# Four of 22 tile lists moved from layer 0 into layer 1's loop, with small steps given to ScalarE and GpSimd

## The chip, the cores and the metric

One core of a Trainium2 chip runs the whole program. The time is that of the device in microseconds, the median of several runs. Engines are named as the profile does: PE is TensorE's matmul and PEld its weight load, DVE is VectorE, ACT ScalarE, POOL GpSimd, SP SyncE, which here only issues transfers.

## The reference, cut to what matters

Four graph layers run one after the other on N = 2708 nodes with D = 128 features and one adjacency matrix `adj` of 2708 x 2708, of which under 1% is not zero. Each layer normalises x, takes the ReLU, and adds its result to x.

```python
# layer 0
msg = jnp.matmul(H.T, X); msg * inv_deg[:, None]
# layer 1
messages = gelu(s[:, None, :] + d[None, :, :] + msg_b)
aggregated = jnp.einsum('ijd,ij->id', messages, adj)
new_feats = concatenate([node_feats, aggregated]) @ upd_w.T + upd_b
# layer 2: adj @ states, then a GRU cell
# layer 3: two heads of attention, masked by adj > 0
```

Layer 1 needs one Gelu for each pair (i, j) and feature, but only where adj[i, j] is not zero.

## The kernel before, in words

The rows are 22 tiles of 128 (the last has 20), in groups of four (`GROUPS`). For layer 1 the columns are cut into 22 blocks of JB = 124. In each block the kernel keeps up to S = 8 entries of each row: `val` (their values) and `col` (their column numbers), made by `max` and `max_index` on VectorE. These are the lists. The diagonal is kept apart: `own` has its values, and `near` is a copy of the two or three blocks around the diagonal with the diagonal set to zero.

**Layer 0** (lines 173 to 234) reads adj tile by tile into `a4`, which holds four tiles and exists twice. For each tile PE adds to the six accumulators `accs`; GpSimd makes `near` and `dg` (the diagonal); VectorE sums `dg` to `own` (L211) and makes the 22 blocks of the list (L216, L217); ScalarE counts the entries by `Sign` (L219). For each group PE transposes 22 x 4 squares (L225), ScalarE evacuates them to `aT` and sums them into `sums` (L229), and SP stores them in `adjT` (L232) for layer 2. Loads and stores stand in one queue, SP's. The order of the instructions in this part is made by the framework's own scheduler. After it VectorE makes `deg` from `sums` (L239 to L243), which `enter` needs.

**Layer 1** is written out by hand under `manual_schedule`: each engine's queue has the order of the program text. First the steps `enter`, `rows_and_turn`, `turn_rows` and `destinations` bring in the six groups, with the periods -3, -2, -1 between them; then `period(t)` runs for t = 0 to 22, and the rest of `updates`. A period works on several tiles at once, in six steps k = 0 to 5:

- `combine(t, k)`: PE adds source and destination parts of four blocks in a bank `p_m` (two banks); `activate(t, k)`: ScalarE's Gelu (L511); `gather(t, k)`: PE multiplies by `put` and adds to `agg`.
- `put_values(t + 1)`, at the start: GpSimd makes the first HP = 8 blocks of `put` from `mine` and `value` (L423). `put_more(t + 1, k)`: ScalarE makes the other 14 (L431).
- `pass_on(t + 1)` and `columns(t + 1)`: the column numbers go through DRAM and come back spread over the partitions.
- `rank(t + 3)` and `describe(t + 3)`, at k = 1: PE counts (`p_r`), VectorE copies the counts to `ends` and `ends4`; then `split` cuts `val` in three bf16 parts: ScalarE casts (L324), VectorE subtracts (L325, `v_r`), ScalarE casts (L326), GpSimd subtracts (L327).
- `select_rows(t + 3)` at k = 2 compares for `sel` and shifts it by one partition through SP to `later`; `finish_rows(t + 3)` at k = 4 subtracts (L370).
- `fetch(t + 2)` at k = 1 and 2: PE fetches the entries by `sel`; `place(t + 2)` at k = 3: VectorE makes `slot`, `hot`, `picked`, `where`, `value` and `mine`.
- `count_rows(t + 4)` at k = 2 reads the list of tile t + 4: the list has to be there by then.
- `sources` every second period and `updates` in steps over eight periods.

**Layers 2 and 3** follow, with `layer3_weights` making `w_x` and `src_w`. A dense version of all layers stands behind a test and isn't run here.

Of the kernel before, what the change touches and what calls it, by code (L numbers as in the profile page):

```python
# [20 lines left out]
F32 = mybir.dt.float32  # L21
BF16 = mybir.dt.bfloat16
AF = mybir.ActivationFunctionType
ALU = mybir.AluOpType
# [6 lines left out]
P = 128  # L31
# [20 lines left out]
def size(t):  # L52
    return min(P, N - t * P)


def width(b):
    return min(JB, N - b * JB)
# [3 lines left out]
def listed_layers(ctx: ExitStack, tc: tile.TileContext, x, adj, w, out, flag):  # L61
# [8 lines left out]
    def bank(name):  # L70
        return ps.tile([P, CH], F32, tag="ps", name=name)
# [98 lines left out]

    sumT = keep.tile([D, N], F32, name="hT1")
    hT = sumT
    with tc.tile_pool(name="l0c", bufs=1) as fix:
        offdiag = fix.tile([P, P], F32, name="offdiag")
        nc.vector.tensor_scalar(offdiag, ident, -1.0, 1.0, ALU.mult, ALU.add)
        sums = fix.tile([P, NT, len(GROUPS)], F32, name="sums")
        nc.gpsimd.memset(sums, 1.0)
        with (
            tc.tile_pool(name="l0", bufs=2) as rows,
            tc.tile_pool(name="l0k", bufs=2) as pool,  # L180
            tc.tile_pool(name="l0t", bufs=4) as turned,
            tc.tile_pool(name="l0p", bufs=1, space=PSUM) as acc,
        ):
            accs = [acc.tile([P, CH], F32, name=f"acc{c}") for c in range(len(CHUNKS))]
            for gi, (g0, gk) in enumerate(GROUPS):
                i0, iw = span(g0, gk)
                a4 = rows.tile([P, 4, N], F32, name="a")
                if gk < 4:
                    nc.gpsimd.memset(a4[:, gk - 1, :], 0.0)
                for q in range(gk):  # L190
                    n = g0 + q
                    m = size(n)
                    a = a4[:, q, :]
                    nc.sync.dma_start(a[0:m, :], adj[n * P : n * P + m, :])
# [5 lines left out]
                    d0 = n * P  # L200
                    b0 = d0 // JB
                    b1 = (d0 + m - 1) // JB
                    c0, c1 = b0 * JB, min((b1 + 1) * JB, N)
                    near = pool.tile([P, 3 * JB], F32, name="near")
                    nc.gpsimd.tensor_copy(near[:, 0 : c1 - c0], a[:, c0:c1])
                    dg = pool.tile([P, P], F32, name="dg")
                    nc.gpsimd.tensor_tensor(dg[:, 0:m], a[:, d0 : d0 + m], ident[:, 0:m], ALU.mult)
                    nc.gpsimd.tensor_tensor(
                        near[:, d0 - c0 : d0 - c0 + m], a[:, d0 : d0 + m], offdiag[:, 0:m], ALU.mult
                    )  # L210
                    nc.vector.reduce_sum(own[:, n : n + 1], dg[:, 0:m], AX.X)  # L211
                    for b in range(NB):
                        ab = a[:, b * JB : b * JB + width(b)]
                        if b0 <= b <= b1:
                            ab = near[:, b * JB - c0 : b * JB - c0 + width(b)]
                        nc.vector.max(val[:, n, b, :], ab)  # L216
                        nc.vector.max_index(col[:, n, b, :], val[:, n, b, :], ab)  # L217
                    sign = pool.tile([P, N], BF16, name="sign")
                    nc.scalar.activation(sign, a, AF.Sign, accum_out=total[:, n : n + 1])  # L219
                for j in range(NT):  # L220
                    k = size(j)
                    p = bank("p_T")
                    for q in range(gk):
                        m = size(g0 + q)
                        nc.tensor.transpose(  # L225
                            p[0:k, q * P : q * P + m], a4[0:m, q, j * P : j * P + k], ident[0:m, 0:m]
                        )
                    aT = turned.tile([P, CH], F32, name="aT")
                    nc.scalar.activation(  # L229
                        aT[0:k, 0:iw], p[0:k, 0:iw], AF.Copy, accum_out=sums[0:k, j, gi : gi + 1]  # L230
                    )
                    nc.sync.dma_start(adjT[0:k, j, i0 : i0 + iw], aT[0:k, 0:iw])  # L232
# [6 lines left out]
        nc.vector.reduce_sum(dsum, sums, AX.X)  # L239
# [15 lines left out]
    nc.vector.tensor_scalar(half_b, b_hh[:, 2:3], 0.5, None, ALU.mult)  # L255


    NX = 2 * D + 4
    w_x = late.tile([P, NX], F32, name="w_x")
    src_w = late.tile([P, 2, P], F32, name="src_w")  # L260

    def layer3_weights():
        nc.vector.tensor_copy(w_x[:, 0 : 2 * D], ff0T)
        for k in range(2):
            p = bank("p_w")[:, 0:2]
            nc.tensor.matmul(p, ff0[:, k, :], attn[:, 2 * k : 2 * k + 2], start=True, stop=True)
            nc.vector.tensor_copy(w_x[:, 2 * D + k : 2 * D + k + 1], p[:, 1:2])
            nc.vector.tensor_copy(w_x[:, 2 * D + 2 + k : 2 * D + 3 + k], p[:, 0:1])
        for k in range(2):
            nc.vector.tensor_copy(src_w[:, k, :], w_x[:, 2 * D + 2 + k : 2 * D + 3 + k].to_broadcast([P, P]))  # L270

    HB = NB // 2
    HP = 8
    R = 4
    C = 4 * S + R + 1  # L280
    with (
# [2 lines left out]
        tc.tile_pool(name="l1w", bufs=1) as once,  # L284
        tc.tile_pool(name="l1s", bufs=4) as selpool,
        tc.tile_pool(name="l1b", bufs=3) as three,
        tc.tile_pool(name="l1q", bufs=2) as putpool,
        tc.tile_pool(name="l1y", bufs=2, space=PSUM) as ypool,
        tc.tile_pool(name="l1m", bufs=2, space=PSUM) as mpool,
# [29 lines left out]
        for q in range(2):  # L319
            nc.vector.tensor_copy(xb[q][:, :, 4 * S : 4 * S + R], part.unsqueeze(1).to_broadcast([P, NB, R]))  # L320

        def split(dst, src, rest):

            nc.scalar.copy(dst[0], src)  # L324
            nc.vector.tensor_tensor(rest, src, dst[0], ALU.subtract)  # L325
            nc.scalar.copy(dst[1], rest)  # L326
            nc.gpsimd.tensor_tensor(dst[2], rest, dst[1], ALU.subtract)  # L327

# [8 lines left out]
        def compare(dst, numbers, op):  # L337
# [5 lines left out]
                op,  # L343
            )

        def rank(t):
            p = rpool.tile([P, CH], F32, tag="r", name="p_r")
            nc.tensor.matmul(p[:, 0:NB], before, rows_n[:, t, :], start=True, stop=True)
            nc.vector.tensor_copy(ends[:, t, :], p[:, 0:NB])
            nc.vector.tensor_copy(ends4, p[:, 0:NB].unsqueeze(2).to_broadcast([P, NB, R]))  # L350

        def describe(t):
            x = xb[t % 2]
            rest = once.tile([P, NB, S], F32, name="v_r")
            split([x[:, :, q * S : (q + 1) * S] for q in range(3)], val[:, t, :, :], rest)
# [30 lines left out]
        def place(t):  # L386
# [70 lines left out]
        def sources(k):  # L457
# [24 lines left out]
            gs = three.tile([P, 2, D], F32, name="gs")  # L482
# [113 lines left out]
        def period(t):  # L596
# [5 lines left out]
            for k in range(GB):  # L602
# [131 lines left out]
    row = l3.tile([P, 2, N], F32, name="row")  # L734
    score = l3.tile([P, NT, 4], F32, name="score")
    nc.gpsimd.memset(score[:, NT - 1, :], 0.0)
    ident_8 = l3.tile([P, P], U8, name="ident_8")
    nc.vector.tensor_copy(ident_8, ident)
    PIECE = 5
    RUNS = ((0, 3), (3, 8), (11, 8), (19, 3))  # L740
    MOST = 8
# [781 lines left out]
```

## Time and profile before

| | us |
|---|---|
| median of 3 runs | 1118.6 (1118.3 to 1119.38) |
| profiled execution | 1119.5 |
| its span, first to last instruction | 1117.6 |
| PE, PEld busy | 966.6, 763.3 |
| DVE, ACT, POOL busy | 840.2, 504.0, 393.4 |
| layer 0, first load to `deg` | 0.7 to 242.0 |
| entry of layer 1, to PE's first combine | 242.0 to 313.7 |
| loop of layer 1 | 313.7 to 652 |
| layers 2 and 3 | 652 to 1117.6 |

Busy times are sums over the span and overlap between engines. A group's row gives the line, the engine, the operation, the tiles written and read, the number of instructions, the busy time and the mean of one. In a timeline the columns are the start in us, the length, the engine and line; a bracket has the idle time ahead of the instruction and what ended it. In a list of waits they are the total in us, the number and the longest.

### The profile page before, as it was taken

The numbers are of one execution on the slowest core, as the hardware profiler recorded it, in microseconds if no ns is written. First come the engines' busy times: TensorE is split into PE (matmuls) and PEld (weight loads), VectorE is DVE, ScalarE is ACT, GpSimd is POOL, SyncE is SP. The second block draws the span as 40 slices with busy tenths as digits, with TensorE's granted clock in tenths as the row PEclk, the third lists the DMA queues.
The fourth block names the chain that finished last, engine by engine and source line by source line (L and its number), as shares of the span: only waits on it lengthen the run. The fifth ranks groups of instructions, "written<-read, shape, count | busy, mean of one in ns | idle before, by whom it ended". The sixth has DMA issues, their size and how long they took to land. (4 is left out here: it accounts for less than half of the span.)

```text
span 1117.6 us, 21914 instructions
## 1 busy us (share of the span) xinstructions
PE 966.6 (86%) x7968; PEld 763.3 (68%) x7968; DVE 840.2 (75%) x2948; ACT 504.0 (45%) x1319; POOL 393.4 (35%) x466
## 2 busy tenths in 40 slices
PE   3988887932489999999999988999979999999993
PEld 1554444512379999989898953444468899999772
DVE  5999999997647667687777364656668987997673
ACT  3966656622556666666665631433322200230143
POOL 3111112102546656666665343354301200250132
PEclk9999898755589999999999988999989999999996
DMA  9497886521113332232332046555300000000000
GB/s 357 187 312 261 309 294 241 186 61 51 53 56 102 106 105 102 82 106 79 105 105 79 28 144 211 186 198 199 99 18 1 1 9 1 1 20 1 2 15 14
DMA packets 55298, 125.39 MB, mean 112 GB/s; under 512 B 7414, under 2 KB 19782, under 8 KB 52472
## 3 DMA queue, kind: packets, MB, share of 16 engines
q1 hardware_dynamic: 48590, 121.12, 31.2%
q10 hardware_dynamic: 6590, 2.77, 1.0%
q8 instruction: 64, 1.05, 0.4%
q14 instruction: 54, 0.44, 0.1%
HBM read 77.30 MB, written 30.84 MB: 97 GB/s over the span
## 5 line engine op out<-in xcount | busy, mean ns | idle before, releaser
L804 PE MATMUL att<-hv,wt 128*128 128x129 f32 (+2 forms) x1936 | 240.7, 281 | 9.2 <-DVE wt L772 9.2
L804 PEld LDWEIGHTS att<-hv,wt 128*128 128x128 f32 (+2 forms) x1936 | 221.8, 190 | 26.3 <-DVE wt L772 8.7
L772 DVE SCALAR_TENSOR_TENSOR wt<-row,lift,mask 128x1024 f32<-128x1024 f32 (+5 forms) x176 | 160.0, 939 | 34.2 <-PE att L804 34.1
L423 POOL TENSOR_SCALAR put<-mine,value 128x128 f32<-128x128 bf16 x176 | 144.8, 839 | 74.2 <-DVE mine L339 71.8
L499 PE MATMUL p_m<-s,sel 128*128 128x128 bf16 x1452 | 161.9, 220 | 7.7 <-ACT g L511 4.7
L503 PE MATMUL p_m<-d,cols 124*128 124x128 bf16 (+1 forms) x1452 | 161.7, 219 | 1.4 <-DVE cols L453 1.3
L119 POOL TENSOR_TENSOR n_r<-n_r,minus_half 128x4 f32<-128x4 f32 (+1 forms) x36 | 48.3, 1343 | 298.5 <-DVE n_r L118 289.6
L196 PE MATMUL acc<-a,hs 128*128 128x512 f32 (+2 forms) x264 | 122.3, 599 | 24.7 <-DMA a<-in_adj 17.9
L524 PE MATMUL agg<-put,g 128*128 128x128 f32 (+1 forms) x968 | 135.9, 281 | 0.0
L925 PE MATMUL p_agg<-a,hs 128*128 128x512 f32 (+2 forms) x264 | 111.1, 562 | 8.2 <-DVE u L572 4.1
L524 PEld LDWEIGHTS agg<-put,g 128*128 128x128 f32 x968 | 118.2, 192 | 0.0
L217 DVE FIND_INDEX8 col<-val,a 128x8 uint16<-128x124 f32 (+1 forms) x441 | 117.9, 278 | 0.0
L499 PEld LDWEIGHTS <-sel 128*128 128x128 bf16 x1452 | 104.1, 98 | 13.3 <-issue 9.5
L503 PEld LDWEIGHTS <-cols 124*128 124x128 bf16 (+1 forms) x1452 | 102.3, 98 | 2.5 <-DVE cols L453 1.9
L511 ACT ACTIVATE g<-p_m 128x512 f32<-128x512 f32 x132 | 73.0, 553 | 65.6 <-PE p_m L503 64.5
L216 DVE MAX8 val<-a 128x8 f32<-128x124 f32 (+1 forms) x441 | 101.8, 269 | 0.0
L431 ACT ACTIVATE put<-mine,value 128x128 f32<-128x128 bf16 x308 | 100.5, 390 | 0.0
L225 PEld LDWEIGHTS p_T<-ident,a 128*128 128x128 f32 x484 | 59.6, 147 | 56.3 <-ACT aT L229 27.0
L196 PEld LDWEIGHTS acc<-a,hs 128*128 128x128 f32 (+1 forms) x264 | 49.4, 207 | 69.0 <-issue 41.8
L225 PE MATMUL p_T<-ident,a 128*128 128x128 f32 x484 | 78.4, 295 | 20.8 <-DMA a<-in_adj 10.2
L229 ACT ACTIVATE aT<-p_T 128x512 f32<-128x512 f32 (+2 forms) x132 | 70.9, 540 | 43.6 <-issue 16.8
L925 PEld LDWEIGHTS p_agg<-a,hs 128*128 128x128 f32 (+1 forms) x264 | 48.5, 196 | 57.0 <-issue 56.0
(228 smaller groups left out, 1407.1 us busy)
## 6 DMA issues: line engine op xcount, KB each, us to landing
a<-in_adj SPq DMA_DIRECT2D x21, 1354.0 KB
adjT<-aT SPq DMA_DIRECT2D x105, 256.0 KB
a<-adjT SPq DMA_DIRECT2D x20, 1280.0 KB
spread<-passed SPq DMA_DIRECT2D x22, 704.0 KB
later<-sel SPq DMA_DIRECT2D x22, 616.0 KB
later<-sel SPq DMA_DIRECT2D x22, 82.5 KB
adjT<-aT SPq DMA_DIRECT2D x21, 74.0 KB
a<-adjT SPq DMA_DIRECT2D x4, 370.0 KB
```

The lines of the kernel that those rows point to most:

```text
L196: nc.tensor.matmul(accs[ci][:, 0:cw], h[0:m, n, :], a[0:m, c : c + cw], start=(n == 0), stop=(n == NT - 1))
L216: nc.vector.max(val[:, n, b, :], ab)
L217: nc.vector.max_index(col[:, n, b, :], val[:, n, b, :], ab)
L225: nc.tensor.transpose(p[0:k, q * P : q * P + m], a4[0:m, q, j * P : j * P + k], ident[0:m, 0:m])
L423: nc.gpsimd.tensor_scalar(st["put", 0][:, b, :], st["mine"][:, b, :], st["value"][:, b : b + 1], None, ALU.mult)
L431: nc.scalar.activation(st["put", 1][:, b - HP, :], st["mine"][:, b, :], AF.Identity, scale=st["value"][:, b : b + 1])
L499: nc.tensor.matmul(p[:, b - b0, :], st["sel"][:, b, :], s3[:, q, t % 2, :], start=(q == 0), stop=False)
L503: nc.tensor.matmul(p[:, b - b0, :], st["cols"][0:kb, b, :], d3[0:kb, b, q, :], start=False, stop=(q == 2))
L524: nc.tensor.matmul(agg, g[:, b - 4 * k, :], put, start=(b == 0), stop=False)
L772: nc.vector.scalar_tensor_tensor(wt[0:kj, :], row[0:kj, k, c : c + n], lift[0:kj, j, k : k + 1], mask[0:kj, j, c : c + n], op0=ALU.max, op ...
L804: nc.tensor.matmul(banks[s // 3][0:m, s % 3, :], wt[0:kj, q * P : q * P + m], hv[0:kj, j, k, :], start=(v < 2 and s // 3 not in touched), ...
L925: nc.tensor.matmul(pa[:, 0:n], h[0:k, j, :], a[0:k, j - j0, 0:n], start=(j == 0), stop=(j == NT - 1))
```

## The change

The tiles n in `LATER` = (8, 12, 16, 20) are loaded and used in layer 0 as before, but their lists, `near` and `own` are left out there. In layer 1's loop the same rows of adj are read a second time, a quarter of a tile's columns in each of the periods' preparations: `load_late(t + 1)` at k = 3 issues the loads on SP, `list_late(t, k)` makes one block of the list at the end of each k and the rest at k = 5. With the fourth quarter `near1` is loaded too and `take_out` runs on it at once. In periods 0 to 15 there are five or six blocks each.

`take_out` serves both places. The diagonal's sum to `own`, so far VectorE's, is now a ScalarE copy with an accumulator, for all 22 tiles. The copies to `ends` and `ends4` and the step `slot` go from VectorE to ScalarE; the subtraction `v_r` in `describe` goes to GpSimd (`narrow`). HP goes from 8 to 7, so ScalarE makes 15 blocks of `put`. `s3` and `gs` have two buffers and not three; `w_x`, `src_w` and `offdiag` lie in other pools.

```diff
+    LATER = (8, 12, 16, 20)
+    def take_out(n, near, diagonal, pool):
+        m = size(n)
+        d0 = n * P - near_blocks(n)[0] * JB
+        dg = pool.tile([P, P], F32, name="dg")
+        nc.gpsimd.tensor_tensor(dg[:, 0:m], diagonal, ident[:, 0:m], ALU.mult)
+        nc.gpsimd.tensor_tensor(near[:, d0 : d0 + m], diagonal, offdiag[:, 0:m], ALU.mult)
+        nc.scalar.activation(dg[:, 0:m], dg[:, 0:m], AF.Copy, accum_out=own[:, n : n + 1])
+    def list_block(n, b, ab):
+        nc.vector.max(val[:, n, b, :], ab)
+        nc.vector.max_index(col[:, n, b, :], val[:, n, b, :], ab)
...
-                    nc.vector.reduce_sum(own[:, n : n + 1], dg[:, 0:m], AX.X)
-                    for b in range(NB):
+                    if n not in LATER:
...
+                        take_out(n, near, a[:, d0 : d0 + m], pool)
+                        for b in range(NB):
...
-    HP = 8
+    HP = 7
...
-        def split(dst, src, rest):
+        def split(dst, src, rest, narrow=False):
             nc.scalar.copy(dst[0], src)
-            nc.vector.tensor_tensor(rest, src, dst[0], ALU.subtract)
+            (nc.gpsimd if narrow else nc.vector).tensor_tensor(rest, src, dst[0], ALU.subtract)
             nc.scalar.copy(dst[1], rest)
             nc.gpsimd.tensor_tensor(dst[2], rest, dst[1], ALU.subtract)
...
+        late_lists = {}
+        for i, n in enumerate(LATER):
+            b0, b1 = near_blocks(n)
+            others = [b for b in range(NB) if not b0 <= b <= b1]
+            cuts = (0, 6, 11, 17, len(others))
+            for q in range(4):
+                late_lists[4 * i + q] = (n, others[cuts[q] : cuts[q + 1]], range(b0, b1 + 1) if q == 3 else ())
+        def load_late(t):
+            if t not in late_lists:
+                return
+            n, blocks, close = late_lists[t]
+            part_a = work.tile([P, 6 * JB], F32, name="part_a")
...
+                    nc.sync.dma_start(part_a[:, i0 * JB : i0 * JB + cw], adj[n * P : (n + 1) * P, c : c + cw])
+            if close:
...
+                near = once.tile([P, 3 * JB], F32, name="near1")
+                nc.sync.dma_start(near[:, 0 : c1 - c0], adj[n * P : (n + 1) * P, c0:c1])
+                take_out(n, near, near[:, d0 : d0 + P], once)
...
+        def list_late(t, k):
+            units = state.get(("late", t), [])
+            for _ in range(len(units) if k == GB - 1 else min(1, len(units))):
+                list_block(*units.pop(0))
...
-            nc.vector.tensor_copy(ends[:, t, :], p[:, 0:NB])
-            nc.vector.tensor_copy(ends4, p[:, 0:NB].unsqueeze(2).to_broadcast([P, NB, R]))
+            nc.scalar.copy(ends[:, t, :], p[:, 0:NB])
+            nc.scalar.copy(ends4, p[:, 0:NB].unsqueeze(2).to_broadcast([P, NB, R]))
...
-            nc.vector.tensor_scalar(slot, lead[:, :, R], part, -1.0, ALU.subtract, ALU.mult)
+            nc.scalar.activation(slot, lead[:, :, R], AF.Identity, bias=part, scale=-1.0)
...
-            s3 = three.tile([P, 3, 2, D], BF16, name="s3")
+            s3 = two.tile([P, 3, 2, D], BF16, name="s3")
...
+                if k == 3:
+                    load_late(t + 1)
+                list_late(t, k)
```

More of the change, by code (lines that the diff above doesn't have):

```diff
@@ L172, in listed_layers, with near_blocks @@
     hT = sumT
+    offdiag = keep.tile([P, P], F32, name="offdiag")
+    nc.vector.tensor_scalar(offdiag, ident, -1.0, 1.0, ALU.mult, ALU.add)
+    LATER = (8, 12, 16, 20)
+    def near_blocks(n):
+        return n * P // JB, (n * P + size(n) - 1) // JB
+    def take_out(n, near, diagonal, pool):
[8 more added lines that the diff above has]
+        nc.vector.max_index(col[:, n, b, :], val[:, n, b, :], ab)
     with tc.tile_pool(name="l0c", bufs=1) as fix:
-        offdiag = fix.tile([P, P], F32, name="offdiag")
-        nc.vector.tensor_scalar(offdiag, ident, -1.0, 1.0, ALU.mult, ALU.add)
         sums = fix.tile([P, NT, len(GROUPS)], F32, name="sums")
@@ L198, in listed_layers @@
                         )
[L200 to L210, printed above, removed]
-                    nc.vector.reduce_sum(own[:, n : n + 1], dg[:, 0:m], AX.X)
-                    for b in range(NB):
[L213 to L217, printed above, removed]
+                    if n not in LATER:
+                        d0 = n * P
+                        b0, b1 = near_blocks(n)
+                        c0, c1 = b0 * JB, min((b1 + 1) * JB, N)
+                        near = pool.tile([P, 3 * JB], F32, name="near")
+                        nc.gpsimd.tensor_copy(near[:, 0 : c1 - c0], a[:, c0:c1])
+                        take_out(n, near, a[:, d0 : d0 + m], pool)
+                        for b in range(NB):
+                            ab = a[:, b * JB : b * JB + width(b)]
+                            if b0 <= b <= b1:
+                                ab = near[:, b * JB - c0 : b * JB - c0 + width(b)]
+                            list_block(n, b, ab)
                     sign = pool.tile([P, N], BF16, name="sign")
@@ L255, in listed_layers @@
     nc.vector.tensor_scalar(half_b, b_hh[:, 2:3], 0.5, None, ALU.mult)
[L258 to L270, printed above, removed]
     HB = NB // 2
-    HP = 8
+    HP = 7
     R = 4
@@ L286, in listed_layers @@
         tc.tile_pool(name="l1b", bufs=3) as three,
+        tc.tile_pool(name="l1d", bufs=2) as two,
         tc.tile_pool(name="l1q", bufs=2) as putpool,
@@ L344, in compare @@
             )
+        late_lists = {}
+        for i, n in enumerate(LATER):
+            b0, b1 = near_blocks(n)
+            others = [b for b in range(NB) if not b0 <= b <= b1]
[7 more added lines that the diff above has]
+            part_a = work.tile([P, 6 * JB], F32, name="part_a")
+            units = []
+            for i, b in enumerate(blocks):
+                units.append((n, b, part_a[:, i * JB : i * JB + width(b)]))
+            cut = next((i for i in range(1, len(blocks)) if blocks[i] != blocks[i - 1] + 1), len(blocks))
+            for i0, i1 in ((0, cut), (cut, len(blocks))):
+                if i1 > i0:
+                    c, cw = blocks[i0] * JB, (i1 - i0 - 1) * JB + width(blocks[i1 - 1])
+                    nc.sync.dma_start(part_a[:, i0 * JB : i0 * JB + cw], adj[n * P : (n + 1) * P, c : c + cw])
+            if close:
+                c0, c1 = close[0] * JB, min((close[-1] + 1) * JB, N)
+                d0 = n * P - c0
+                near = once.tile([P, 3 * JB], F32, name="near1")
+                nc.sync.dma_start(near[:, 0 : c1 - c0], adj[n * P : (n + 1) * P, c0:c1])
+                take_out(n, near, near[:, d0 : d0 + P], once)
+                units += [(n, b, near[:, b * JB - c0 : b * JB - c0 + width(b)]) for b in close]
+            state["late", t] = units
+        def list_late(t, k):
+            units = state.get(("late", t), [])
+            for _ in range(len(units) if k == GB - 1 else min(1, len(units))):
+                list_block(*units.pop(0))
         def rank(t):
@@ L354, in describe @@
             rest = once.tile([P, NB, S], F32, name="v_r")
-            split([x[:, :, q * S : (q + 1) * S] for q in range(3)], val[:, t, :, :], rest)
+            split([x[:, :, q * S : (q + 1) * S] for q in range(3)], val[:, t, :, :], rest, True)
             nc.gpsimd.tensor_copy(x[:, :, 3 * S : 4 * S], col[:, t, :, :])
@@ L478, in sources @@
                     nc.vector.tensor_tensor(sb[0:mq, q, :, :], pv[0:mq, q, :, :], bv[0:mq, :, :], ALU.add)
-            s3 = three.tile([P, 3, 2, D], BF16, name="s3")
+            s3 = two.tile([P, 3, 2, D], BF16, name="s3")
             rest = once.tile([P, 2, D], F32, name="s_r")
             split([s3[:, q, :, :] for q in range(3)], sb[:, :, 0, :], rest)
-            gs = three.tile([P, 2, D], F32, name="gs")
+            gs = two.tile([P, 2, D], F32, name="gs")
             nc.scalar.activation(gs, sb[:, :, 1, :], AF.Gelu)
@@ L736, in listed_layers, with layer3_weights @@
     nc.gpsimd.memset(score[:, NT - 1, :], 0.0)
+    NX = 2 * D + 4
+    w_x = l3.tile([P, NX], F32, name="w_x")
+    src_w = l3.tile([P, 2, P], F32, name="src_w")
     ident_8 = l3.tile([P, P], U8, name="ident_8")
     nc.vector.tensor_copy(ident_8, ident)
+    def layer3_weights():
+        nc.vector.tensor_copy(w_x[:, 0 : 2 * D], ff0T)
+        for k in range(2):
+            p = bank("p_w")[:, 0:2]
+            nc.tensor.matmul(p, ff0[:, k, :], attn[:, 2 * k : 2 * k + 2], start=True, stop=True)
+            nc.vector.tensor_copy(w_x[:, 2 * D + k : 2 * D + k + 1], p[:, 1:2])
+            nc.vector.tensor_copy(w_x[:, 2 * D + 2 + k : 2 * D + 3 + k], p[:, 0:1])
+        for k in range(2):
+            nc.vector.tensor_copy(src_w[:, k, :], w_x[:, 2 * D + 2 + k : 2 * D + 3 + k].to_broadcast([P, P]))
     PIECE = 5
```

## The prediction

> **What bounds the kernel now.** I read the busy times by stage first, then in layer 0 who waited for whom and the engines' timelines at its end, then the timelines of one period of layer 1's loop. The stages, with columns PE, PEld, DVE, ACT, POOL busy (instructions), clock, DMA share, GB/s:
>
> ```profile
> 100.00:140.00 40.00, 33.65 (x146) 19.61 (x145) 40.00 (x270) 25.04 (x56) 5.20 (x12) 0.93 0.83 290
> 214.00:243.00 29.00, 16.00 (x65) 9.91 (x64) 28.90 (x196) 11.62 (x56) 0.50 (x2) 0.62 0.34 110
> 243.00:314.00 71.00, 24.60 (x137) 19.92 (x138) 50.66 (x159) 25.44 (x68) 27.43 (x33) 0.52 0.15 48
> 314.00:652.00 338.00, 327.74 (x4523) 315.82 (x4522) 233.00 (x456) 216.75 (x624) 202.90 (x252) 0.99 0.26 88
> ```
>
> In layer 0 VectorE (DVE) never rests: it makes the lists. In the loop (314 to 652) TensorE (PE) is busy 327.7 of 338, and DVE only 233. So work moved from the first to the second looks free. Two questions decide: what ends layer 0 when DVE's lists no longer do, and whether the loop has slack in the order of its queues, not only in its sums. The waits of SP's queue, then ACT's last evacuations and DVE's last list:
>
> ```profile
> SPq L232 <- ACT aT L229: 146.1, 116, 26.3
> SPq L194 <- POOL a L189: 7.5, 1, 7.5
> ...
> 233.76 0.28 ACT L229 ACTIVATE aT<-p_T 20x148 f32<-20x148 f32 x1
> 233.95 0.19 ACT L229 ACTIVATION_READ_ACCUMULATOR aT<-p_T 20x1 f32 x1
> ...
> 241.44 0.25 DVE L217 FIND_INDEX8 col<-val,near 128x8 uint16<-128x104 f32 x1
> ...
> 242.03 0.28 DVE L239 TENSOR_REDUCE deg<-sums 128x22 f32<-128x132 f32 x1
> ```
>
> SP's loads (L194) stand in one queue with the stores of the turned tiles (L232), which wait for ACT; DVE appears in no long wait of SP. So the chain load, transpose, evacuate, store runs at its own pace (the first loads of successive groups are issued at 65.9, 106.8, 144.3, 183.2 us: 39 us a group) and ends at 234.1, only 7.9 us before `deg` starts. `deg` reads `sums`, which those evacuations write.
>
> One period of the loop (ACT, POOL, DVE):
>
> ```profile
> 449.00 1.61 DVE L339 TENSOR_TENSOR mine<-count_h,lead 128x2816 bf16<-128x2816 bf16 x1
> 450.81 8.03 POOL L423 TENSOR_SCALAR put<-mine,value 128x128 f32<-128x128 bf16 x8 [6.43 <-DVE mine L339]
> 453.26 0.47 DVE L325 TENSOR_TENSOR v_r<-val,xb 128x176 f32<-128x176 f32 x1 [0.87 <-ACT xb L324]
> 453.77 0.37 ACT L326 CAST xb<-v_r 128x176 bf16<-128x176 f32 x1 [0.61 <-DVE v_r L325]
> 454.62 0.57 ACT L511 ACTIVATE g<-p_m 128x512 f32<-128x512 f32 x1
> 458.81 0.54 POOL L327 TENSOR_TENSOR xb<-v_r,xb 128x176 bf16<-128x176 f32 x1
> ```
>
> POOL starts its eight puts when DVE has made `mine`, and is occupied until 458.84. In the midst, at 453.3, DVE makes `v_r`, ACT takes it half a microsecond later, and goes on to the Gelu that empties PE's bank.
>
> **What the Trainium skill says.** "Perfetto Trace Analysis", section Tensor Engine Instruction: ACT, DVE and GpSimd are strict FIFO; a waiting instruction holds all behind it. The trace agrees: L327 stands behind the puts for 5 us though its input was there at 454.1. "SBUF — State Buffer", section SBUF: two separate sides: DVE and GpSimd lock a port pair for a whole instruction, if DVE runs in a two-port mode or reads two SBUF inputs. The trace agrees: a put takes 0.595 us at least and 2.09 at most, and eight take 5.9 us when they meet one of the 1.6 us bf16 comparisons or subtractions, 7.8 to 8.4 when two. `max` and `max_index` have one input each: I expect no such stall from them.
>
> **The change, part by part.**
>
> 1. *Lists leave layer 0.* Two blocks of `max` and `max_index` take 0.89 us from start to start (236.32 to 237.21), so 0.445 each, 22 a tile, four tiles: 39.2 us off DVE. Row L211 (`own`, 22 x 0.258) takes off 5.7 more. DVE would end at about 241.7 - 44.9 = 197. But `deg` waits for ACT's last evacuation at 234.1, so the gain is 242.0 - 234.2 = **7.8 us**, unless that chain shortens. It can a little: SP stood 7.5 us before the last load, for a memset (L189) that lies in POOL's queue behind `dg` and `near`, and these wait for DVE (166.3 us in that stage, POOL otherwise idle). With DVE lighter this wait goes; I take 5 of the 7.5. Against it: `own` goes to ACT, 18 x (0.29 + 0.19, the narrow evacuation and its accumulator read) = 8.6 us, which now waits for POOL's `dg` and so for DVE's pace. ACT idles 28 us there before `sign`, waiting for loads, so most is hidden; I take 3 as lost. Sum **-10 us**. Bounds: +5 (ACT held behind DVE) to -33 (all down to the last load's landing at 199 plus one tile of lists, 10 us). The stretch 243 to 314 keeps its order and length; it begins earlier.
>
> 2. *The lists in the loop.* 39.2 us over 16 periods, 2.5 each; `ends`, `ends4`, `slot`, `v_r` (rows 3.9 + 5.3 + 5.9 + 8.3 = 23.4) leave. DVE comes to 233 + 39 - 23 = 249 of 338: no bound by sum. Its waits for `p_r` (20.6 us) and `v_r` (14.9) go too, so it absorbs the units; cost 0. If that cover fails, `sel` (L370) comes late and PE waits at L380 (3.0 us in all now).
>
> 3. *Second loads.* 5.5 MB in 16 periods, SP 1 to 3 issues of 0.3 to 0.5 us; SP is mostly idle, and DMA is 26% busy. They are issued a period (15.3 us) ahead of their use; 1.35 MB landed within 10 us in layer 0. They stand behind `later` and before `passed` on SP: cost 0. The exception is `near1` in periods 2, 6, 10, 14: `take_out` follows its load at once, so POOL's `dg` and then ACT's `own` wait for it. The "DMA: Bandwidth & Descriptors" page of the Trainium skill, section Anatomy of one DMA, gives about 2 us fixed; the trace agrees (`passed`, 5.5 KB, issued 449.75, its reader issued 451.76). Behind `later` and the part I reckon 3 us from issue; ACT waits 2 to 4 us with the Gelus behind it, some 1.5 reach PE: 4 x 1.5 = **+6 us** (bounds 0, +16).
>
> 4. *`ends`, `ends4`, `slot` and a fifteenth put on ACT.* Taken at their DVE durations, 9.2 + 5.9, and 22 x 0.33 = 7.3: ACT goes from 217 to about 243 of 338 with the own's, no bound by sum. The p_r bank is freed behind a Gelu instead of by DVE: both come near 452.2 here, 0.
>
> 5. *`v_r` on POOL.* This is what I hold decisive. In program order it stands behind the seven puts, and ACT's L326 behind it. With today's times the puts would end in this period at 450.8 + 7/8 x 8.03 = 457.8, `v_r` at 458.4; ACT, at L326 since 453.2, stands 5.2 us, 4.6 more than now. The same sum for the other periods (puts' start, 7/8 of their time, plus 0.54, against L326) gives 46 us over 18 periods: 2.5 to 6 us in eleven of them, under 2 in the others. Behind L326 stand three puts and the Gelu of bank k = 2. PE has two `p_m` banks, and about 3.8 us of work before it needs that one back (rest of the combines 1.4, gathers 2 x 1.0, fetch 0.3), so a stall of 5 us reaches PE with 1 to 3 us, the late Gelus behind it included.
> With `slot` on ACT it closes into a ring that every period must go round: `mine`, seven puts (5.1 to 6.9 by the rows above, mean 6.0), `v_r` 0.54, ACT from L326 to `slot` (0.37, nine puts at 0.30, two Gelus at 0.5, lead 0.1, slot 0.25 = 4.4; sources 1.9 every second period and the update's 0.6 + 1.65 + 1.65 every fourth, mean 1.9), then DVE's hot to `mine` (446.77 to 450.61, 3.8), and some 0.3 for semaphores: 16.9 us. The loop now goes at 15.3 (L324 from 320.3 to 594.9, 18 periods). So 1.6 x 18, rounded to **+30 us**. Bounds: 0 (5.1 for the puts, and sources and update not in the ring's way: 14.2, under the present period) and +54 (7.3 for the puts in every period: 18.3).
>
> 6. *At nothing:* `s3` and `gs` with two buffers: the pair before is released by `close_tile` at k = 1, ahead of `sources` at k = 2. `w_x`, `src_w`, `offdiag` move in memory only; layer 3's helper is called at the same place.
>
> Sum: -10 + 6 + 30 = **+26 us**. The profiled execution took 1119.5 us (span 1117.6), the median of the runs is 1118.6, 0.9 less; 1119.5 + 26 is 1145.5, and on the scale of the median 1144.6. I say **1145**.
>
> **The rivals.**
> - *A, faster: POOL is done before ACT asks.* If `mine` ends some 6.5 us or more before ACT comes to L326, there is no stall. DVE is freed of the waits for `p_r` and `v_r` and could run ahead. Against it: it gets 2.5 us of lists in the same period, and in the period shown `mine` ends at 450.6, 2.6 us before ACT reaches L326. Then -10 + 6 gives 1115, and with layer 0 at its full -33, 1092.
> - *B, DVE's order binds as well:* four or five list units lie between `sel`'s subtraction and the next comparison, 2 us; fetch waits at L380, 1.3 us more in 16 periods, +21: 1166.
> - *C, layer 0 gives nothing:* ACT's `own` holds `sign` and the evacuations at DVE's pace, +5 in place of -10: 1160.
> - *D, the move to layer 1 is not what the automatic order of layer 0 makes of it:* the queues of layer 0 are ordered anew, loads come earlier and 20 of the 33 us are gained: 1135.
>
> **How the numbers follow.** Forecast 0.50 (its own range 1128 to 1162), A 0.17, B 0.13, C 0.10, D 0.10. A gives faster 0.15 and 0.02 no change; a forecast at its lowest ends gives 0.01 and 0.01. Under 0.2% (2.2 us) a measurement of this kernel can't tell from no change. Faster 0.16, same 0.03, slower 0.81. The range reaches into A on one side and past B on the other: 1110 to 1172.
>
> **What would show it.** Right: DVE's lists end near 200 to 210 and `deg` starts at 225 to 236; in the loop L326 on ACT waits for POOL `v_r`, 40 to 80 us in all, PE's waits at L499 for ACT's Gelu rise from 4.7 us to 30 or more, periods become 16.5 to 18 us up to the eighteenth, and those after are as now. ACT's `own` waits for `dg` four times. Wrong: `v_r` waits short, with PE still near 97% busy in the loop; or the first combine before 290 us.

## The result and the profile after

The changed kernel takes **1156.95 us** (median of 4 runs, 1155.9 to 1159.5) against 1118.8 beside it: ratio 1.0344, 95% interval 1.0326 to 1.0363, or 38 us slower. The profiled execution has a span of 1157.7 us where that of before has 1117.6. The changed code has other line numbers: own on ScalarE is L188, max and max_index L191 and L192, the load L213, evacuation and store L241 and L244, `v_r` L323 between the casts L322 and L324, put L459, combine L535 and L539, Gelu L547.

The stages again, columns as before (PE, PEld, DVE, ACT, POOL, clock, DMA share, GB/s):

```profile
210.00:240.00 30.00, 27.10 (x98) 15.93 (x97) 3.80 (x27) 18.94 (x72) 0.00 (x0) 0.67 0.43 153
240.00:314.00 74.00, 23.32 (x135) 18.64 (x135) 47.57 (x146) 26.29 (x78) 25.81 (x32) 0.55 0.18 57
314.00:690.00 376.00, 334.66 (x4484) 320.20 (x4484) 261.23 (x634) 226.73 (x709) 196.12 (x260) 0.96 0.28 92
```

DVE is busy 3.8 of 30 us at the end of layer 0, where before it had no rest: the lists did leave. In the loop no engine is full by its sum, but PE, which was busy in 97% of the stage before, is down to 89%. The end of layer 0, in the timeline of the changed kernel:

```profile
213.53 0.27 DVE L192 FIND_INDEX8 col<-val,near 128x8 uint16<-128x104 f32 x1
...
241.92 0.25 DVE L331 TENSOR_SCALAR some<-val 128x176 bf16<-128x176 f32 x1 [28.12 <-ACT aT L241]
...
242.10 0.18 ACT L241 ACTIVATION_READ_ACCUMULATOR aT<-p_T 20x1 f32 x1
242.32 0.29 DVE L251 TENSOR_REDUCE deg<-sums 128x22 f32<-128x132 f32 x1
```

DVE's last list ends 28 us earlier than before (213.8 for 241.7), and `deg` starts at 242.3 for 242.0. DVE stands 28.12 us for the last evacuation, which now ends at 242.3 and not 234.1. The gain of layer 0 is not small, it is nil.

The waits in the loop (324 to 668 us; total, number, longest):

```profile
ACT xb L324 <- POOL v_r L323: 52.0, 19, 4.8
...
PE p_m L535 <- ACT g L547: 32.3, 16, 6.5
...
DVE hot L429 <- ACT slot L427: 24.0, 10, 5.0
...
ACT dg L188 <- POOL dg L186: 17.7, 4, 6.3
POOL dg L186 <- DMA near<-in_adj: 13.3, 4, 6.3
```

The same two waits in the loop of the kernel before (314 to 652 us):

```profile
ACT xb L326 <- DVE v_r L325: 10.3, 19, 0.8
...
PE p_m L499 <- ACT g L511: 4.7, 6, 1.6
```

ACT's two waits ahead of the Gelus are those that the forecast names: `v_r` 19 times, `own` four times. One ordinary period (POOL, ACT, DVE):

```profile
409.58 6.69 POOL L459 TENSOR_SCALAR put<-mine,value 128x128 f32<-128x128 bf16 x7 [5.93 <-DVE mine L337]
416.24 0.53 POOL L323 TENSOR_TENSOR v_r<-val,xb 128x176 f32<-128x176 f32 x1
416.80 0.37 ACT L324 CAST xb<-v_r 128x176 bf16<-128x176 f32 x1 [4.09 <-POOL v_r L323]
417.94 0.57 ACT L547 ACTIVATE g<-p_m 128x512 f32<-128x512 f32 x1
420.74 0.33 ACT L427 ACTIVATE slot<-lead,part 128x22 f32<-128x22 bf16 x1
421.10 0.34 DVE L429 TENSOR_TENSOR hot<-count,slot 128x176 f32<-128x176 f32 x1 [2.26 <-ACT slot L427]
423.33 1.61 DVE L337 TENSOR_TENSOR mine<-count_h,lead 128x2816 bf16<-128x2816 bf16 x1
425.12 5.30 POOL L459 TENSOR_SCALAR put<-mine,value 128x128 f32<-128x128 bf16 x7 [6.15 <-DVE mine L337]
```

This is the ring in one view: `mine`, seven puts, `v_r`, the cast, then, by way of ACT's queue (without a gap from the cast on), `slot`, for which DVE waits, and `mine` again. From put to put it takes 15.54 us here.

But the periods, from PE's `p_w` matmul of one to the next, put most of the loss elsewhere. From `p_w` 0 to `p_w` 20 the loop takes 343.5 us, before 304.9. The four periods with `near1` rise by 9.6, 7.2, 6.8 and 4.1 us (the first from 14.9 to 24.5), 27.7 of the 38.6; the sixteen others by 10.9 together, 0.7 each. (Entry and loop together are 44.5 us longer, the span only 40.1: what follows the loop takes 490.6 us and not 495.0. It is shorter, 490.4 to 493.5, in every kernel with four late lists; why stays open.) The first `near1` in the timeline:

```profile
366.65 0.33 PE L535 MATMUL p_m<-s,sel 128*128 128x128 bf16 x3 [0.76 <-ACT g L547]
...
367.92 0.45 SPq L371 DMA_DIRECT2D near<-in_adj  x1
...
372.09 1.60 DVE L406 TENSOR_TENSOR sel<-sel,later 128x2816 bf16<-128x2816 bf16 x1
372.12 1.89 POOL L186 TENSOR_TENSOR dg<-near,ident 128x128 f32<-128x128 f32 x1 [6.29 <-DMA near<-in_adj]
...
374.04 0.31 ACT L188 ACTIVATE dg<-dg 128x128 f32<-128x128 f32 x1 [6.34 <-POOL dg L186]
...
374.35 0.58 ACT L547 ACTIVATE g<-p_m 128x512 f32<-128x512 f32 x1
...
374.98 0.48 PE L535 MATMUL p_m<-s,sel 128*128 128x128 bf16 x3 [6.55 <-ACT g L547]
...
375.57 0.53 PE L535 MATMUL p_m<-s,sel 128*128 128x128 bf16 x3
```

From the load's issue to POOL's start it takes 4.2 us here, in the three later cases 3.0, 3.8 and 3.0. Then POOL's multiplication, 0.455 us in layer 0 of the kernel before (L207), meets DVE's subtraction and takes 1.89; later it takes 1.49, 0.45 and 0.45. All 6.3 us of ACT's wait arrive at PE.

The wait costs more than its length. Behind it three matmuls of a combine take 0.53 us where they took 0.33, and the clock granted to PE is halved (columns as in the stages):

```profile
366.00:373.50 7.50, 1.78 (x20) 1.61 (x20) 7.36 (x15) 1.71 (x6) 1.38 (x1) 1.00 0.46 139
373.60:380.30 6.70, 5.32 (x40) 4.98 (x40) 2.30 (x13) 3.75 (x12) 4.92 (x9) 0.50 0.00 0
380.40:387.00 6.60, 6.60 (x110) 6.57 (x109) 4.02 (x7) 3.79 (x14) 2.98 (x4) 1.00 0.55 193
```

The loop's 4137 matmuls keep PE busy for 306.5 us, before for 295.8. So 10.7 of the loop's 38.6 us are slower matmuls and 27.7 are waits (36.7 for 9.0). The forecast priced waits alone.

### The profile page after: what moved, and what is told of

The parts are those of the page before. It is cut to its first block, busy times and chain, and to the rows that moved or that the text cites. A ratio compares the mean times of both kernels' runs of the same rounds, so it can differ in the third digit from the quotient of the medians.

```text
span 1157.7 us, 21972 instructions
## 1 busy us (share of the span) xinstructions
PE 979.2 (85%) x7968; PEld 771.7 (67%) x7968; DVE 823.6 (71%) x2838; ACT 521.5 (45%) x1451; POOL 382.0 (33%) x462
## 5 line engine op out<-in xcount | busy, mean ns | idle before, releaser
L535 PE MATMUL p_m<-s,sel 128*128 128x128 bf16 x1452 | 164.8, 223 | 35.4 <-ACT g L547 32.3
L539 PE MATMUL p_m<-d,cols 124*128 124x128 bf16 (+1 forms) x1452 | 164.8, 223 | 0.2
L459 POOL TENSOR_SCALAR put<-mine,value 128x128 f32<-128x128 bf16 x154 | 121.9, 807 | 87.3 <-DVE mine L337 66.2
L560 PE MATMUL agg<-put,g 128*128 128x128 f32 (+1 forms) x968 | 139.1, 286 | 0.0
L535 PEld LDWEIGHTS <-sel 128*128 128x128 bf16 x1452 | 106.3, 99 | 42.7 <-issue 38.9
L560 PEld LDWEIGHTS agg<-put,g 128*128 128x128 f32 x968 | 121.3, 196 | 0.0
L467 ACT ACTIVATE put<-mine,value 128x128 f32<-128x128 bf16 x330 | 107.3, 392 | 0.0
L539 PEld LDWEIGHTS <-cols 124*128 124x128 bf16 (+1 forms) x1452 | 104.8, 99 | 1.2 <-issue 0.7
L237 PE MATMUL p_T<-ident,a 128*128 128x128 f32 x484 | 81.4, 302 | 26.3 <-ACT aT L241 15.9
L192 DVE FIND_INDEX8 col<-val,a 128x8 uint16<-128x124 f32 x361 | 96.0, 274 | 0.0
L547 ACT ACTIVATE g<-p_m 128x512 f32<-128x512 f32 x132 | 72.6, 550 | 49.6 <-PE p_m L539 47.4
L191 DVE MAX8 val<-a 128x8 f32<-128x124 f32 x361 | 82.9, 265 | 15.2 <-DMA a<-in_adj 15.2
L241 ACT ACTIVATE aT<-p_T 128x512 f32<-128x512 f32 (+2 forms) x132 | 71.0, 541 | 38.6 <-issue 18.5
```

Source lines behind the costliest of these rows:

```text
L237: nc.tensor.transpose(p[0:k, q * P : q * P + m], a4[0:m, q, j * P : j * P + k], ident[0:m, 0:m])
L459: nc.gpsimd.tensor_scalar(st["put", 0][:, b, :], st["mine"][:, b, :], st["value"][:, b : b + 1], None, ALU.mult)
L467: nc.scalar.activation(st["put", 1][:, b - HP, :], st["mine"][:, b, :], AF.Identity, scale=st["value"][:, b : b + 1])
L535: nc.tensor.matmul(p[:, b - b0, :], st["sel"][:, b, :], s3[:, q, t % 2, :], start=(q == 0), stop=False)
L539: nc.tensor.matmul(p[:, b - b0, :], st["cols"][0:kb, b, :], d3[0:kb, b, q, :], start=False, stop=(q == 2))
L560: nc.tensor.matmul(agg, g[:, b - 4 * k, :], put, start=(b == 0), stop=False)
```

## The experiments

All twelve were timed beside the kernel before, which stayed at 1118.9 us. Entry is the start of the first `p_w`, loop from there to the twentieth after it; both, and the end of the last evacuation (evac), are from the one profiled execution of each, where a median is over 4 to 20 runs. In several of the kernels whose layer 0 DVE no longer ends, single runs differ by 9 to 14 us (`b2_three` 1113.5 to 1122.6, and its profiled execution is the fastest), so totals below are from medians and the stages only show where.

| run | median | ratio, 95% interval | evac | entry | loop |
|---|---|---|---|---|---|
| before | 1118.8 | | 234.1 | 317.7 | 304.9 |
| after | 1156.95 | 1.0344 (1.0326 to 1.0363) | 242.3 | 323.7 | 343.5 |
| a1_near_early | 1147.1 | 1.0250 (1.0233 to 1.0267) | 240.3 | 322.3 | 335.3 |
| a2_vr_vector | 1142.8 | 1.0230 (1.0204 to 1.0255) | 236.4 | 310.4 | 337.5 |
| a3_own_vector | 1150.6 | 1.0268 (1.0234 to 1.0302) | 235.3 | 317.2 | 344.5 |
| a4_vr_alone | 1150.3 | 1.0287 (1.0270 to 1.0304) | 235.4 | 320.1 | 333.4 |
| b1_lists_alone | 1137.0 | 1.0157 (1.0138 to 1.0175) | 227.0 | 302.0 | 333.2 |
| b2_three | 1119.1 | 1.0000 (0.9983 to 1.0016) | 226.1 | 300.0 | 319.3 |
| b3_steps_back_near | 1122.95 | 1.0030 (1.0013 to 1.0047) | 236.1 | 312.5 | 319.7 |
| b4_slot_back | 1119.8 | 1.0020 (0.9994 to 1.0046) | 229.7 | 304.3 | 319.0 |
| e1_two_late | 1114.7 | 0.9960 (0.9938 to 0.9981) | 234.5 | 310.7 | 309.3 |
| e2_one_late | 1113.9 | 0.9957 (0.9942 to 0.9972) | 233.6 | 309.2 | 306.6 |
| e3_own_scalar | 1129.65 | 1.0078 (1.0053 to 1.0104) | 243.0 | 318.1 | 318.6 |
| e4_vr_first | 1119.2 | 1.0003 (0.9994 to 1.0012) | 235.0 | 317.9 | 305.6 |

### One part of the change undone

**a1_near_early**: `near1` is loaded with the third quarter, a period ahead of `take_out`.

```diff
+            if t % 4 == 2:
+                state["near"] = once.tile([P, 3 * JB], F32, name="near1")
+                nc.sync.dma_start(state["near"][:, 0 : c1 - c0], adj[n * P : (n + 1) * P, c0:c1])
...
-                nc.sync.dma_start(near[:, 0 : c1 - c0], adj[n * P : (n + 1) * P, c0:c1])
+                near = state.pop("near")
```

> The changed kernel (1157), with near1's load issued one period earlier, in the call for the third quarter and not the fourth; take_out stays where it is, so its input has landed some 15 us before. Theory F (the forecast): the ring through v_r costs 30 us of the loop and the wait for near1 6, so 1151. Theory N (from the trace after: the four periods with take_out are 9.6, 7.2, 6.8 and 4.1 us longer than before, 27.7 of the loop's 38.6): 24 us or more go, 1130 to 1134, and the four periods become 16 to 17 us.

9.9 us less, between the two theories. The first two of the four long periods shrink from 24.5 and 22.6 to 16.0 and 16.2 us; the later two stay at 21.2 and 19.5. And ACT's waits for `v_r` rise from 52.0 to 59.1 us, as they would if one wait had hidden part of the other.

**a2_vr_vector**: `v_r` back on DVE.

```diff
-            split([...], val[:, t, :, :], rest, True)
+            split([...], val[:, t, :, :], rest)
```

> The changed kernel with the subtraction v_r back on VectorE, all else the same. Theory F: the ring opens, 25 to 30 us go, 1127 to 1132. Theory N: the ring costs only the 11 us by which the sixteen other periods are longer, so 8 to 11 go, 1146 to 1149, and the four periods with take_out stay at 20 to 24 us.

14.2 us less, again between the two. In the profiled executions the loop gives 5.9, and 7.4 lie ahead of it: from the last evacuation to the first `p_w` it takes 73.9 us, with `v_r` on POOL 81.4 in the changed kernel. Another 5.9 lie in layer 0, which this edit does not touch; this execution is the fastest of four that differ by 6.2 us. The `own` waits stay: ACT stands 18.2 us for `dg` four times.

**a3_own_vector**: in layer 0 the sum of the diagonal back on DVE.

```diff
+        if early:
+            nc.vector.reduce_sum(own[:, n : n + 1], dg[:, 0:m], AX.X)
+        else:
             nc.scalar.activation(dg[:, 0:m], dg[:, 0:m], AF.Copy, accum_out=own[:, n : n + 1])
```

> The changed kernel with the sum of the diagonal (own) of the 18 tiles of layer 0 back on VectorE; in the loop it stays on ScalarE. Theory F: ScalarE's own costs 3 us in layer 0, 1154. Theory N (in the trace after, ScalarE stands 5.5 us at 101 to 106.5 for POOL's dg, which is held by near and so by VectorE's lists, and the load of tile 12 is issued at 112.8 and not 106.8): layer 0's last evacuation comes back from 242 to 234 or before, 8 to 12 us go, 1145 to 1149.

6.4 us less, in layer 0 alone: the last evacuation ends at 235.3, the loop (344.5) is as in the changed kernel.

**b2_three**: a1, a2 and a3 in one.

> The changed kernel with three parts mended together: near1 loaded a period earlier, v_r on VectorE, own of layer 0 on VectorE. Theory H: both stalls are gone, the loop comes back to 305 to 313 us from 343, layer 0 ends near 235: 1112 to 1122, within 0.4% of the kernel before. Theory U: VectorE's list units hold the loop by themselves, at 16 to 17 us a period: 1130 or more.

1119.1 us, no different from before, though the loop, at 319.3 us, did not come back to the 305 to 313 expected. The three together hold the whole loss: 38 us, where their single gains add to 30.4.

### One part alone

**a4_vr_alone**: the kernel before with `v_r` on POOL, all else as it was (HP = 8).

```diff
-            nc.vector.tensor_tensor(rest, src, dst[0], ALU.subtract)
+            (nc.gpsimd if narrow else nc.vector).tensor_tensor(rest, src, dst[0], ALU.subtract)
```

> The kernel before (1118.6), with the subtraction v_r on GpSimd and nothing else (eight puts, slot on VectorE, no second lists). Theory F: eight puts stand ahead of it, ScalarE stalls 2.5 to 6 us in eleven periods; 14 to 28 us slower, 1133 to 1147. Theory N: the stall reaches PE with less than 1 us a period, 5 to 10 slower, 1124 to 1129.

1150.3 us, 31.5 more and above both theories. ACT's wait, from the waits of this run's loop and its timeline:

```profile
ACT xb L326 <- POOL v_r L325: 61.1, 19, 6.6
```
```profile
344.07 0.53 POOL L325 TENSOR_TENSOR v_r<-val,xb 128x176 f32<-128x176 f32 x1
344.63 0.37 ACT L326 CAST xb<-v_r 128x176 bf16<-128x176 f32 x1 [5.67 <-POOL v_r L325]
...
345.47 0.57 ACT L511 ACTIVATE g<-p_m 128x512 f32<-128x512 f32 x1
...
346.10 0.33 PE L499 MATMUL p_m<-s,sel 128*128 128x128 bf16 x3 [2.77 <-ACT g L511]
```

An instruction of 0.53 us, moved between two engines with room, costs 28.5 us in the loop: 16.7 us a period. PE's waits for Gelu rise by 18.3 us (23.0 for 4.7), and its matmuls take 10.2 longer (306.0 for 295.8).

**e4_vr_first**: the same, but the puts are issued behind `describe`, so that `v_r` stands ahead of them in POOL's queue.

```diff
-            if c:
-                put_values(t + 1)
...
                 if k == 1 and a:
                     describe(t + 3)
+                if k == 1 and c:
+                    put_values(t + 1)
```

> The run a4_vr_alone (kernel before with v_r on GpSimd alone, 1150 us) with put_values(t + 1) issued after describe at k = 1 and not ahead of it, so that v_r stands before the eight puts in GpSimd's queue. Theory (the cost is the place in the queue, behind the puts, not the engine): ScalarE's wait for v_r falls from 61 us to under 20, the loop from 333 to 305 to 312, 1118 to 1128 us. Rival (GpSimd is too slow or too full in the loop for this step wherever it stands, or the puts made later hold the gathers): loop over 325, 1140 or more.

```profile
439.69 0.53 POOL L325 TENSOR_TENSOR v_r<-val,xb 128x176 f32<-128x176 f32 x1 [3.50 <-ACT xb L324]
440.70 0.54 POOL L327 TENSOR_TENSOR xb<-v_r,xb 128x176 bf16<-128x176 f32 x1 [0.48 <-ACT xb L326]
...
441.65 6.90 POOL L423 TENSOR_SCALAR put<-mine,value 128x128 f32<-128x128 bf16 x8
```

1119.2 us. Now POOL waits for ACT, 98.2 us in all, ACT for `v_r` 19.1, and PE for Gelu 5.1; puts that start later hold up nobody. The cost was the place in the queue, not the engine.

**b1_lists_alone**: the kernel before with late lists, second loads and late `take_out`; layer 0's own, `ends`, `slot`, `v_r` and HP as before; the pools are the changed kernel's. **b3_steps_back_near**: the same with `near1` loaded a period ahead, by the edit of a1.

> The kernel before with the late lists and nothing else of the change: own of layer 0, ends, ends4, slot and v_r on VectorE, eight puts on GpSimd; near1 is loaded as in the change, so the take_out of the four late tiles waits for it. If the two stalls hide behind each other (theory H: taking one away from the changed kernel brought only 10 or 14 us because the other then came forward), the wait for near1 stands here alone at its full size, 20 to 27 us, against a layer 0 that is 7 us shorter: 1132 to 1140. If list units on VectorE bind the loop too (theory U), 1143 or more.

> The late lists with near1 loaded a period earlier and every small step (own of layer 0, ends, ends4, slot, v_r, the eighth put) back where it was before. Theory H: 1110 to 1118, at or under the kernel before; against the lists alone with the late near1 this is the price of that wait, 20 to 27 us. Theory U: VectorE has 12 us of work in each of the sixteen periods and holds up PE at the fetch: 1125 or more.

1137.0 and 1122.95 us: `near1` by itself costs 14.1 us, 13.6 in the loop. b3 came out between its two theories. Against before its entry is 5.2 us earlier and its loop 14.8 longer. The busy times of b3 in periods 0 to 7 and 8 to 15, then of before in periods 8 to 15 (columns as in the stages):

```profile
312.50:432.50 120.00, 117.06 (x1643) 113.06 (x1642) 101.13 (x260) 75.61 (x227) 68.32 (x93) 0.99 0.37 121
432.50:566.60 134.10, 120.79 (x1655) 115.64 (x1654) 118.11 (x322) 81.28 (x240) 81.11 (x104) 0.99 0.32 106
...
434.30:559.70 125.40, 119.70 (x1666) 115.27 (x1664) 94.80 (x190) 81.20 (x236) 81.28 (x100) 1.00 0.28 94
```

In the second half, when `updates` runs as well, DVE is at 88% (before 76%), and there 9.8 of the 14.8 us arise, counted from `p_w` to `p_w`. But this is not the lists alone. Over the whole loop PE waits 6.2 us more for `sel` (9.2 for 3.0) and 5.1 more for Gelu (9.8 for 4.7), and its matmuls take 3.4 longer (299.2 for 295.8): together the 14.8. The wait for Gelu is still that for `own`: in periods 10 and 14 POOL's `dg` stands behind a step of `updates`, and ACT stands 2.6 us each time, all of which reaches PE. So only the waits for `sel`, and a part of the slower matmuls, are the price of the lists themselves.

**b4_slot_back**: b2 with `slot` back on DVE.

```diff
-            nc.scalar.activation(slot, lead[:, :, R], AF.Identity, bias=part, scale=-1.0)
+            nc.vector.tensor_scalar(slot, lead[:, :, R], part, -1.0, ALU.subtract, ALU.mult)
```

> As the kernel with three parts mended, with slot on VectorE as well; only ends, ends4 and the fifteenth put stay moved. If ScalarE's slot is a tie by itself (VectorE's hot waits for it, 24 us in all in the changed kernel), 2 to 6 us go; if it was late only because ScalarE stood at v_r or own, within 2 us of the kernel with three parts mended.

1119.8 us: the place of `slot` can't be told from nothing once `v_r` isn't behind the puts.

**e3_own_scalar**: b2 with layer 0's own on ACT again.

> The run b2_three with one thing set back to the changed kernel: layer 0's sum of the diagonal on ScalarE. Theory (own on ScalarE ties ScalarE's evacuations to GpSimd's dg and so to VectorE, and that alone delays the loads of the groups): last evacuation 4 to 8 us later than b2's 226, first loads of groups 3 and 4 near 112 and 149 in place of 105 to 108 and 142 to 146, first combine 304 to 308, time 1123 to 1127. Rival (it only seemed so, and the delay of layer 0 came from the later stage): as b2, 1117 to 1121.

10.6 us more, above what was expected, and all of it ahead of the loop. How it works, in the timeline of ACT:

```profile
101.01 0.21 ACT L241 ACTIVATION_READ_ACCUMULATOR aT<-p_T 128x1 f32 x1
106.71 0.31 ACT L188 ACTIVATE dg<-dg 128x128 f32<-128x128 f32 x1 [5.49 <-POOL dg L186]
106.93 0.19 ACT L188 ACTIVATION_READ_ACCUMULATOR dg<-dg 128x1 f32 x1
107.02 0.58 ACT L241 ACTIVATE aT<-p_T 128x512 f32<-128x512 f32 x1
```

ACT stops evacuating for 5.5 us because POOL's `dg` waits behind `near` for DVE; SP's stores wait for the evacuations, and the next group's first load goes out at 113.2 us (b2: 104.5; changed kernel: 112.8; before: 106.8). The delay stays: the group after it starts at 149.7, against 140.9.

### A version between

**e1_two_late** and **e2_one_late**: b3 with LATER = (16, 20) and (20,), so that units stand in periods 0 to 7 or 0 to 3.

> The run b3_steps_back_near (late lists of four tiles, near1 loaded a period earlier, all small steps where the kernel before had them) with only two tiles late, LATER = (16, 20), so that list units stand in periods 0 to 7 only. Theory (layer 0's gain is capped by the chain of loads, transposes and evacuations, while the price of the list units in the loop grows with their number, most of it in periods 8 to 16): layer 0 keeps 7 to 10 us of gain, the loop costs 3 to 6 us over before, 1110 to 1118 us. Rival (the price of the list units falls in any eight periods alike): loop +7 and more, layer 0 half its gain, 1118 to 1123.

> The same with one tile late, LATER = (20,), units in periods 0 to 3. Theory: VectorE's lists end near 232 and the last evacuation near 227 to 234, so that 7 to 9 us of layer 0's gain stay, and the loop costs 1 to 3 us: 1111 to 1117. Rival (the gain of layer 0 is in proportion to the lists moved): gain 2 us, loop +3: 1118 to 1121.

1114.7 and 1113.9 us: both beat both kernels, by 4 to 5 us against before. With one tile moved, DVE's lists end just ahead of the last evacuation, which ends at 233.6, and the entry is 8.5 us earlier; the loop pays 1.7. Moving a second tile brings nothing: the entry is 7.1 us earlier, and the loop pays 4.5.

## Why the prediction was right, and where its terms were off

Direction and size came out, with 38 us for a forecast of 26, and the step held decisive, `v_r` behind the puts, is the largest. That the sum came so near is in part luck, since errors of both signs stand in it. The order of b2, e3, a1 and the changed kernel undoes one edit at a time and splits the 38 us by medians:

| step | adds | forecast |
|---|---|---|
| lists moved, `ends`, `slot`, put on ACT (b2) | +0.3 (entry -17.7, loop +14.4 in a fast profile) | -13 (lists), 0 (rest) |
| layer 0's own on ACT (e3) | +10.6 | +3 |
| `v_r` on POOL (a1) | +17.5 | +30 |
| `near1` loaded late (after) | +9.9 | +6 |

**Part 1, layer 0 -10: wrong by its "3 as lost".** The 7.5 us of SP's wait for a memset went (0.2 remain), and with own and `v_r` on DVE the entries come 5 to 18 us earlier than before. But own on ACT isn't 18 x 0.48 us beside idle time: it ties the evacuations to DVE's pace, as rival C had it, and costs 6.4 (a3) to 10.6 us (e3). Up to the entry the changed kernel has lost 5.9 us, which is rival C's +5 and not the -10. That "the stretch 243 to 314 keeps its order and length" was also wrong: it holds casts that wait for `v_r`, too, and from the last evacuation to the first `p_w` takes 81 to 82 us in the changed kernel, a1 and a3, 74 to 77 in a2, b1 to b4 and e3.

**Part 2, the lists "cost 0": wrong.** b3 pays 14.8 us, 6.2 of them as PE's longer waits for `sel`: rival B's place, but under a third of its 21 us; 5.1 are `own`'s. The sum over the whole loop, 249 of 338, hid the fuller half, and the units aren't 0.445 us each: in the loop's timelines of the changed kernel and of b3 successive units start 0.58 to 0.60 us apart, where each unit's value load starts 0.30 us after its own maxima; in layer 0 two blocks are interleaved, and the second's maxima start 0.19 us after the first's. So the units took some 12 us more of DVE than reckoned (an estimate, 88 units of 0.14). That `ends`, `ends4` and `slot` leave DVE, 15.1 of the 23.4 us set against the units, bought nothing in the loop: it takes 319.3 us with them on ACT (b2), 319.7 with them on DVE (b3). The medians are 3.9 us apart in b2's favour, at the edge of what the spread of single runs allows to tell, and in the profiled executions that difference lies in layer 0.

**Part 3, `near1` +6: right mechanism, price too low.** It cost 14.1 us by itself (b1 to b3), 9.9 as the last of four. I reckoned 3 us from issue, and 3.0 to 4.2 were measured. Twice `dg` stood locked out for 1.4 and 1.0 us on top. The term that failed is the 1.5 us of each wait at PE: nothing stood between ACT and PE, so the whole wait arrived there, and the matmuls behind it were slower. In b1 PE's waits for Gelu are 11.6 us longer than in b3, and its matmuls take 5.0 longer. The "DMA: Bandwidth & Descriptors" page of the Trainium skill (section Anatomy of one DMA) gives about 2 us fixed, for transfers that GpSimd issues. SP issued these, 124 KB behind `later` and `part_a` in one queue, so the 3.0 to 4.2 us measured are the price. That DVE and GpSimd lock one another ("SBUF — State Buffer", section SBUF: two separate sides) is seen in the 1.89 us of `dg`, 0.455 without.

**Part 4, at nothing: right** (b2, b4).

**Part 5, `v_r` +30: right for the step alone, wrong as a term of the sum.** Alone it costs 28.5 us in the loop and 31.5 in all. Its loop goes at 16.7 us a period where the ring said 16.9, but a4 has eight puts and `slot` on DVE, which is not quite the forecast's ring. With seven puts and `slot` on ACT, a1 goes at 16.8 us and e3, without the ring, at 15.9. In company it costs 14.2 (a2 to the changed kernel) to 17.5 us (e3 to a1). The ring was put against the old period of 15.3 us, but lists and `near1` had lengthened the periods already, and these numbers fit a ring that costs only what it is longer than the others. After a long `near1` period, too, the next one runs at 13.8 to 14.6 us, as before (13.8 to 14.8), so the ring costs nothing there. That DVE has caught up meanwhile would explain it, but no run separates this. The singles in the loop, 14.8 + 13.6 + 28.5 = 56.9, come to 38.6 together. So the forecast's total is nearer than its terms: 12 to 16 us too much for `v_r` stands against some 20 too little for lists and own and 4 for `near1`.

Of what was to show it, ACT's wait for `v_r` (52.0), PE's for Gelu (32.3) and four waits for `dg` came. Lists ended at 213.8, `deg` at 242.3, later than named, and the periods were not 16.5 to 18 throughout but 14 to 19 with four of 20.3 to 24.5. Rival A is out: ACT waits 2.7 us for each `v_r` (52.0 in 19), where it waits 0.7 in e1, with `v_r` on DVE (13.0 in 19). Rival D is out too: the first loads of the groups came later.

## What to carry to other kernels

A step moved to an idle engine can cost what stands ahead of it in that engine's queue, and not only its duration; look for a place ahead of the long block (a4 and e4: 31 us for where one line stands). Price the parts that act on one loop against one another, as a longest path, and not one after the other against the old period. When PE has to wait, look at how long its matmuls take afterwards, too. When work is moved to take one engine off the end of a stage, move only until the next chain ends it: here one of the four tiles took all the net gain, the rest only paid.

## What the runs showed of the hardware

- The load of `near1`, 124 KB, issued behind 700 KB of `later` and a part of the same tile within 2.6 us, took 4.2 us from its issue to the first reader, in a stage with the DMA engines 28% busy; the three later ones took 3.0, 3.8 and 3.0.
- After a wait of 6.55 us PE was granted half its clock from 373.6 to 380.3 us, and three matmuls of 128x128 took 0.53 us and not 0.33. In the loops of this case the same 4137 matmuls keep PE busy for 295.8 us with 9.0 us of waits (before), 306.0 with 27.3 (a4) and 306.5 with 36.7 (after).
- One unit of `max`, value load and `max_index` over 128 x 124 takes 0.58 to 0.60 us when units follow one another, 0.445 when two are interleaved, on the same engine with the same instructions.
- The kernel before, whose layer 0 is ended by DVE's instruction count, repeats within 0.3%. With the end left to loads, stores and evacuations some kernels spread over 0.8 to 1.3% (b2 1113.5 to 1122.6, b4 1114.7 to 1129.0), but the four runs of the changed kernel, whose layer 0 ends likewise, stay within 0.3%. That the varying time of the transfers is the cause is argued, not shown.
